# Four batches' inverse roots by Newton's steps on GpSimd, statistics tile by tile, and tokens normalized one tick earlier

## The chip, the cores and the metric

The kernel runs on one core of a Trainium2 chip. The metric is the device time of one execution in microseconds (us); the median of several runs counts. The engines are TensorE (PE; its weight loads are listed as PEld), VectorE (DVE), ScalarE (ACT), GpSimd (POOL) and SyncE (SP), which issues the DMAs. Each works through its own instruction queue in order; they wait for one another by semaphores.

## What is computed

Two layers on x of 8 batches x 256 tokens x 256 channels, all in float32: cross-attention with 16 heads of 16, a soft mixture of experts, a second cross-attention with 16 heads of 64, and a channel mix. Each takes a layer norm of x and adds its result to x:

```python
def _layernorm(x, axis=-1, eps=1e-05):
    m = jnp.mean(x, axis=axis, keepdims=True)
    v = jnp.var(x, axis=axis, keepdims=True)
    return (x - m) / jnp.sqrt(v + eps)

x = x + _L0_xattn_ref(_layernorm(x), ctx_768, mask_BxS2_bf1, ...)
x = x + _L0_ffn_ref(_layernorm(x), ...)
x = x + _L1_xattn_ref(_layernorm(x), ctx_768, ...)   # the second attention
x = x + _L1_ffn_ref(_layernorm(x), ...)              # the channel mix

# the channel mix, on xn = _layernorm(x)
x_prev = xn shifted by one token
xr = mu_r * xn + (1 - mu_r) * x_prev;  xk = mu_k * xn + (1 - mu_k) * x_prev
out = sigmoid(xr @ W_r.T) * (square(relu(xk @ W_k.T)) @ W_v.T)
```

The change touches the layer norms of the last two lines only: the normalized tokens that the second attention projects to queries, and the statistics (mean, variance, inverse root) of the channel mix.

## The kernel before

x stays on the chip as 16 tiles of 128 tokens (`x_sb`); batch b has tiles 2b and 2b+1. The four stages follow one another; in the profile the experts end at about 900 us, the second attention runs from about 930 to 1300, and the channel mix follows.

**The second attention** works through 64 steps, one for each batch and pair of heads (`steps1`, L1195). Two steps make a group, so a batch has four groups. The loop over ticks n (L1426) runs a software pipeline: in tick n it emits the scores of group n, the scaling of group n-1, the transposes of group n-2, the values of group n-3, and, after a batch's last group, its output projection (`project`). A batch's 4 ticks are called a block here.

- `scores` (L1217, L1222): PE writes scores to PSUM, VectorE takes their negated maxima `nm`, ScalarE the exponentials `ex`, four of 128x256 for each step, with their sums `z`.
- `norm` (L1233, L1235): VectorE takes the reciprocals `rz`, GpSimd multiplies `ex` by them, 128x1024 at a time.
- `transposes` (L1251): PE transposes `ex`; VectorE copies one half of each step to `et`, ScalarE the other.
- `values` (L1270): PE multiplies by the values, ScalarE copies the result to `ot`.
- `project` (L1283): PE multiplies by the output weights, VectorE adds the result to `x_sb`. With that a batch's rows are final; the projection of batch b is emitted in tick 4b+7.

Between these, each tick emits pieces for the next batch: keys (L1122, L1123: one half copied by ScalarE, the other by VectorE), values (L1187, L1188) and, in the first tick of a block, `xt_piece`: the two tiles of the next batch are normalized on VectorE (`normed`, L177, tile `xh_l1`), transposed on PE (`pt_x`) and copied to `xT` (L1137); four query pieces (L1157) follow over the block.

Three PSUM tiles of 128x512 (tag "mm") go round among transposes, keys, values, queries and projections, so a PE instruction that starts a new one waits until the copy that read the tile three turns earlier is done.

**Statistics of the channel mix.** `bn_stats` and `bn_aggr` on VectorE give a tile's mean and variance. For the first four batches `ln_half(0, ...)` is emitted at tick 20: eight pairs (L117, L118), one square root with epsilon as bias on ScalarE (L120), one reciprocal on VectorE (L121). The exponentials and the square root need different tables on ScalarE, so a table load stands ahead of the root and another ahead of the next exponential. For batches 4 to 6 `rest_of_stats(4, 3)` does the same at tick 33 (L1415 to L1421), and `rest_of_stats(7, 1)` after the loop. The mix itself (`channel_mix`) begins with `normed` (tile `xh_ffn`) and transposes.

**What sets the order.** The framework does not keep the order of emission: its scheduler orders each engine's queue by its own estimate of when operands are ready. Only what stands in `tc.keep_in_program_order` (PE's matmuls and transposes through `matmul` and `transpose`, `rz`, the roots at L1419) keeps its place. In the built program of before, the pairs of `bn_stats` and `bn_aggr` of batches 0 to 3 stand apart in VectorE's queue, each batch's after its projection's add, and the `xh_ffn` tiles of batches 0 and 1 follow soon after the reciprocal.

Of the kernel before, what the change touches and what calls it, by code (L numbers as in the profile page):

```python
# [7 lines left out]

F32 = mybir.dt.float32
U8 = mybir.dt.uint8  # L10
AF = mybir.ActivationFunctionType
ALU = mybir.AluOpType
AX = mybir.AxisListType

P = 128
B, S, D, C = 8, 256, 256, 192
# [6 lines left out]
EPS = 1e-5  # L23
# [39 lines left out]
def kernel(ctx: ExitStack, tc: tile.TileContext, a: dict, out: bass.AP):  # L63
    nc = tc.nc

    const = ctx.enter_context(tc.tile_pool(name="const", bufs=1))
    stat = ctx.enter_context(tc.tile_pool(name="stat", bufs=2))
# [25 lines left out]
    x_sb = const.tile([P, NT, D], F32, name="x_sb")  # L93
# [7 lines left out]
    epsb = const.tile([P, 1], F32, name="epsb")  # L101
# [7 lines left out]
            a["x"][P * n : P * (n + of), :].rearrange("(t p) d -> p t d", p=P),  # L109
        )  # L110

    def ln_half(half, name):

        mv = stat.tile([P, 8, 2], F32, tag="mv", name=f"mv_{name}")
        for i in range(8):
            st = stat.tile([P, 6], F32, tag="bst", bufs=4, name=f"bst_{name}_{i}")
            nc.vector.bn_stats(st, x_sb[:, half * 8 + i, :])  # L117
            nc.vector.bn_aggr(mv[:, i, :], st)  # L118
        rstd = stat.tile([P, 8], F32, tag="rstd", name=f"rstd_{name}")
        nc.scalar.activation(rstd, mv[:, :, 1], AF.Sqrt, bias=epsb)  # L120
        nc.vector.reciprocal(rstd, rstd)  # L121
        return mv, rstd

    def ln_tiles(n, of, name):

        mv = stat.tile([P, 4, 2], F32, tag="mvp", bufs=4, name=f"mvp_{name}")
        for i in range(of):
            st = stat.tile([P, 6], F32, tag="bst", bufs=4, name=f"bst_{name}_{i}")
            tc.keep_in_program_order(nc.vector.bn_stats(st, x_sb[:, n + i, :]))
            nc.vector.bn_aggr(mv[:, i, :], st)  # L130
        rstd = stat.tile([P, 4], F32, tag="rstdp", bufs=4, name=f"rstdp_{name}")
        nc.scalar.activation(rstd[:, :of], mv[:, :of, 1], AF.Sqrt, bias=epsb)
        nc.vector.reciprocal(rstd[:, :of], rstd[:, :of])
        return mv, rstd

    def ln_pair(p, name):
        return ln_tiles(4 * p, 4, name)
# [34 lines left out]
    def normed(b, mv, scl, name, of=8):  # L172

        xh = work.tile([P, 2, D], F32, tag="xh", bufs=3, name=f"xh_{name}_{b}")
        for t in range(2):
            i = (2 * b + t) % of
            nc.vector.tensor_scalar(  # L177
                xh[:, t, :],
                x_sb[:, 2 * b + t, :],
                mv[:, i, 0:1],  # L180
                scl[:, i : i + 1],
                ALU.subtract,
                ALU.mult,
            )
        return xh

    def transposed(xh, name, turn=None):

        pt = ps_mm(f"pt_{name}")
        for c in range(2):  # L190
            for t in range(2):
                (turn or free_transpose)(
                    pt[:, c * 256 + t * P : c * 256 + (t + 1) * P],
                    xh[:, t, c * P : (c + 1) * P])
        return pt.rearrange("p (c n) -> p c n", c=2)
# [27 lines left out]
    with ExitStack() as l0:  # L223
# [376 lines left out]
        for p in range(1, 4):  # L600
            h, b = 16 * (p - 1), 2 * p
# [160 lines left out]
        for b, plan in enumerate(  # L762
# [8 lines left out]
            for step in plan.split():  # L771
                when, _, args = step[1:].partition(".")
# [3 lines left out]
        turn_back, halves = None, []  # L776
        for h in range(8 * B + 12):
            q, k = [
                (i // 8, i % 8 // 2, i % 2) if 0 <= i < 8 * B else None for i in (h, h - 6)
            ]  # L780
# [284 lines left out]
    with ExitStack() as l1:  # L1065
# [61 lines left out]
        def proj1(b):  # L1127

            to = {}

            def xt_piece():
                mv, rstd = xat_stats[b // 2]
                pt = transposed(normed(b, mv, rstd, "l1", of=4), f"x1_{b}", transpose)
                to["xT"] = p1.tile([P, 2, S], F32, tag="xT", bufs=1, name=f"xT1_{b}")
                nc.vector.tensor_copy(to["xT"], pt)  # L1137
                for t in range(2):
                    nc.gpsimd.tensor_tensor(
                        x_sb[:, 2 * b + t, :], x_sb[:, 2 * b + t, :], bo, ALU.add  # L1140
                    )

            def q_piece(t2):
                if t2 == 0:
                    to["QT"] = p1.tile([P, 8, S], F32, tag="QT", bufs=2, name=f"QT1_{b}")
                pq = ps_mm(f"q1_{b}_{t2}").rearrange("p (t n) -> p t n", t=2)
                for i in range(2):
                    t = 2 * t2 + i
                    for c in range(2):
                        matmul(  # L1150
                            pq[:, i, :],
                            lhsT=wq[:, c, t * P : (t + 1) * P],
                            rhs=to["xT"][:, c, :],
                            start=(c == 0),
                            stop=(c == 1),
                        )
                nc.vector.tensor_scalar(  # L1157
                    to["QT"][:, 2 * t2 : 2 * t2 + 2, :], pq, HD1**-0.5, None, ALU.mult
                )

            def values_of(u):

                if u == 0:
                    to["V"] = p1.tile([P, 2, DA], F32, tag="V", bufs=2, name=f"V1_{b}")
                pv = [ps_mm(f"v1_{b}_{u}_{h}") for h in range(2)]
                t0 = S * b + u * P
                cols = [slice(h * 512, (h + 1) * 512) for h in range(2)]
                for h in range(2):
                    matmul(
                        pv[h],  # L1170
                        lhsT=ctx0T[:, t0 : t0 + P],
                        rhs=wv[:, 0, cols[h]],
                        start=True,
                        stop=False,
                    )

                def halves():
                    for h in range(2):
                        r = slice(64 * h, 64 * h + 64)
                        matmul(  # L1180
                            pv[h],
                            lhsT=ctx1T[r, t0 : t0 + P],
                            rhs=wv[r, 1, cols[h]],
                            start=False,
                            stop=True,
                        )
                    nc.scalar.copy(to["V"][:, u, cols[0]], pv[0])  # L1187
                    nc.vector.tensor_copy(to["V"][:, u, cols[1]], pv[1])  # L1188

                return halves  # L1190

            qs = [[xt_piece]] + [[lambda t=t: q_piece(t) for t in ts] for ts in ((0,), (1,), (2, 3))]
            return to, qs, [lambda u=u: values_of(u) for u in range(2)]

        def steps1(b, to):  # L1195

# [101 lines left out]
                if k < len(step):  # L1298
                    step[k]()

        to, qs, vs = projs[0]
        for t2 in range(4):
            keys(0, t2)()
        for v in vs:
# [4 lines left out]

        ffn_stats = {}
        homes = []

        def homes_of_mix():
# [8 lines left out]
        def channel_mix(b):  # L1324
# [81 lines left out]

            return mix, mixed_keys, mixed_values


        def rest_of_stats(b, of):  # L1410
            mv = stat.tile([P, 8, 2], F32, tag="mv", name=f"mv_ffn_{b}")
            rstd = stat.tile([P, 8], F32, tag="rstd", name=f"rstd_ffn_{b}")
            for i in range(2 * of):
                st = stat.tile([P, 6], F32, tag="bst", bufs=4, name=f"bst_ffn_{b}_{i}")
                nc.vector.bn_stats(st, x_sb[:, 2 * b + i, :])  # L1415
                nc.vector.bn_aggr(mv[:, (2 * b + i) % 8, :], st)
            part = slice(2 * b % 8, 2 * b % 8 + 2 * of)
            tc.keep_in_program_order(
                nc.scalar.activation(rstd[:, part], mv[:, part, 1], AF.Sqrt, bias=epsb)  # L1419
            )  # L1420
            nc.vector.reciprocal(rstd[:, part], rstd[:, part])  # L1421
            for k in range(b, b + of):
                ffn_stats[k] = mv, rstd, 8

        mixes = [channel_mix(b) for b in range(B)]
        for n in range(len(groups) + 4):  # L1426
            b, i = n // 4 + 1, n % 4
            stage(3, n - 3)
            if b < B:
                for piece in projs[b][1][i]:  # L1430
                    piece()
            stage(4, n - 4)
            stage(2, n - 2)
            stage(1, n - 1)


            if i < 2 and n // 8 < B // 2 - 1:
                keys(n // 8 + 1, n % 8 // 4 * 2 + i)()
            elif i >= 2 and b < B:
                projs[b][2][i - 2]()()  # L1440
            stage(0, n)
            if n == 20:
                mv, rstd = ln_half(0, "ffn_0")
                for k in range(4):
                    ffn_stats[k] = mv, rstd, 8
            if n == 33:
                homes_of_mix()
                mixes[0][0]()
                rest_of_stats(4, 3)
            if n == 34:  # L1450
                mixes[1][0]()
        rest_of_stats(7, 1)
        for k in range(1, B + 2):
            for i in range(3):
# [64 lines left out]
```

## Time and profile before

| | us |
|---|---|
| three runs without profiler | 1360.43, 1361.24, 1363.24 |
| their median | 1361.24 |
| the profiled execution | 1366.39 |
| its span, first to last instruction | 1364.6 |
| busy in it: TensorE | 1324.8 |
| VectorE | 571.0 |
| ScalarE | 582.0 |
| GpSimd | 192.8 |
| 69 table loads on ScalarE, each | 1.283 |

The mean granted clock of TensorE in the profiled execution was 0.989 of full speed. Times of single instructions below are those of the profiled execution, counted from the start of its span. A line of a timeline gives start, duration, engine, source line, operation, output<-inputs, shapes, how many instructions are merged in it, and in brackets how long the engine stood idle before it and for whom.

### The profile page before, as it was taken

How to read it: one execution, taken by the hardware profiler on the slowest of the kernel's cores; microseconds unless marked ns; L12 is line 12 of the kernel's file. 1: busy time of each engine (PE TensorE's matmuls, PEld its weight loads, DVE VectorE, ACT ScalarE, POOL GpSimd, SP SyncE). 2: the span in 40 equal slices, each digit the busy share in tenths (PEclk: the TensorE clock that was granted, in tenths of full speed). 3: DMA queues.
4: the chain of work that ended last, by engine and by line, in shares of the span. 5: the costliest groups of instructions: out<-in, count | busy, mean ns of one | idle time of the engine just before them, and what ended most of it. 6: DMA issues, size and time to landing. Idle time of an engine off the chain costs nothing.

```text
span 1364.6 us, 18968 instructions
## 1 busy us (share of the span) xinstructions
PE 1324.8 (97%) x7504; PEld 958.8 (70%) x7504; DVE 571.0 (42%) x1160; ACT 582.0 (43%) x1403; POOL 192.8 (14%) x142
## 2 busy tenths in 40 slices
PE   7998999899999999999999999999999999999998
PEld 3565565467678877778777788875666676677777
DVE  6577776523331133321333110015445444544565
ACT  2455444626342164522545222213536445444663
POOL 1000001101010000100001000002333323323433
PEclk8999998999999999999999999999999999999999
DMA  7100000023243324233233324450000000000001
GB/s 219 57 1 2 1 1 1 1 97 132 66 132 131 127 71 131 93 106 130 80 117 131 111 87 153 144 150 1 1 1 1 1 1 1 1 1 1 2 8 54
DMA packets 59128, 86.84 MB, mean 64 GB/s; under 512 B 3360, under 2 KB 49056, under 8 KB 59040
## 3 DMA queue, kind: packets, MB, share of 16 engines
q1 hardware_dynamic: 58464, 85.11, 19.2%
q8 instruction: 59, 0.97, 0.3%
q10 hardware_dynamic: 576, 0.52, 0.1%
q14 instruction: 29, 0.24, 0.1%
HBM read 83.53 MB, written 2.10 MB: 63 GB/s over the span
## 4 chain that ended last, share of the span: by engine, by line
PE 87%; ACT 6%; DVE 5%; issue 1%; DMA 0%; POOL 0%; ACTq 0%; SPq 0%; DVEq 0%; POOLq 0%
PE ph L968 16%; PE pe L984 16%; PE sc L73 8%; PE q L73 6%; PE o L73 5%; PE k L73 5%; PE po L73 5%; PE pc L1010 4%; PE pe L76 4%; PE v L73 4%; PE pf L914 3%; PE ln L832 3%; ACT ex L1222 2%; PE pf L73 1%; ACT ex L501 1%; DVE NM L490 1%
## 5 line engine op out<-in xcount | busy, mean ns | idle before, releaser
L976 ACT ACTIVATE ht<-ph,b 128x256 f32<-128x256 f32 x256 | 119.1, 473 | 372.1 <-PE ph L968 371.7
L968 PE MATMUL ph<-slots,w 128*128 128x256 f32 x1024 | 266.9, 384 | 0.9 <-ACT ht L976 0.2
L984 PE MATMUL pe<-w,ht 128*128 128x256 f32 x1024 | 263.3, 381 | 0.0
L968 PEld LDWEIGHTS ph<-slots,w 128*128 128x128 f32 x1024 | 182.3, 189 | 54.5 <-ACT ht L976 21.8
L984 PEld LDWEIGHTS pe<-w,ht 128*128 128x128 f32 x1024 | 192.0, 190 | 29.9 <-DVE slots L993 4.3
L1235 POOL TENSOR_TENSOR ex<-ex,rz 128x1024 f32<-128x1024 f32 x64 | 120.1, 1897 | 224.2 <-DVE rz L1233 214.0
L1222 ACT ACTIVATE ex<-sc,nm 128x256 f32<-128x256 f32 x256 | 117.2, 483 | 45.5 <-DVE nm L1217 45.5
L501 ACT ACTIVATE ex<-sc 128x512 f32<-128x512 f32 x128 | 74.7, 596 | 86.6 <-PE sc L73 76.1
L73 PE MATMUL sc<-KT,QT 17*128 17x256 f32 (+1 forms) x1024 | 105.3, 385 | 2.1 <-ACT QT L445 1.5
L490 DVE TENSOR_REDUCE NM<-sc 128x2 f32<-128x512 f32 x128 | 86.6, 687 | 41.4 <-PE sc L73 36.9
L993 DVE TENSOR_TENSOR slots<-pe,b 128x512 f32<-128x512 f32 x32 | 22.1, 691 | 185.4 <-PE pe L984 185.4
L73 PE MATMUL q<-xT,wq 128*128 128x256 f32 x384 | 94.8, 395 | 0.9 <-ACT V L1187 0.9
L73 PEld LDWEIGHTS sc<-KT,QT 17*128 17x128 f32 (+1 forms) x1024 | 77.4, 189 | 25.4 <-issue 15.9
L73 PEld LDWEIGHTS q<-xT,wq 128*128 128x128 f32 x384 | 70.9, 192 | 26.4 <-issue 12.9
L892 POOL TENSOR_TENSOR es<-es,zs 128x1024 f32<-128x1024 f32 x12 | 22.7, 1892 | 445.6 <-DVE zs L891 445.6
L1217 DVE TENSOR_REDUCE nm<-sc 128x4 f32<-128x1024 f32 x64 | 75.3, 1218 | 6.5 <-PE sc L73 2.8
L73 PE MATMUL po<-wo,ot 128*128 128x256 f32 x320 | 72.5, 382 | 0.0
L76 PE MATMUL pe<-ident,ex 128*128 128x128 f32 x512 | 69.9, 278 | 0.5 <-DVE xT L1137 0.4
L73 PEld LDWEIGHTS po<-wo,ot 128*128 128x128 f32 x320 | 60.1, 190 | 10.9 <-issue 3.2
L1251 ACT COPY et<-pe 128x512 f32<-128x512 f32 x64 | 37.0, 607 | 71.9 <-PE pe L76 71.5
L76 PEld LDWEIGHTS pe<-ident,ex 128*128 128x128 f32 x512 | 56.2, 140 | 14.0 <-issue 8.0
L73 PE MATMUL o<-et,V 128*64 128x256 f32 x512 | 62.8, 386 | 0.9 <-ACT ot L1270 0.9
(194 smaller groups left out, 1636.8 us busy)
## 6 DMA issues: line engine op xcount, KB each, us to landing
w<-in_w_dram SPq DMA_DIRECT2D x64, 1024.0 KB, 7.0
b<-in_b_dram SPq DMA_DIRECT2D x32, 128.0 KB, 6.8
x_sb<-in_x_dram SPq DMA_DIRECT2D x3, 512.0 KB, 7.3
ctx0T<-in_ctxT_dram SPq DMA_DIRECT2D x4, 256.0 KB, 8.4
ctx1T<-in_ctxT_dram SPq DMA_DIRECT2D x8, 128.0 KB, 6.9
se<-in_slots_dram SPq DMA_DIRECT2D x1, 1024.0 KB, 5.7
wq<-in_wq_dram SPq DMA_DIRECT2D x1, 1024.0 KB, 4.9
wo<-in_wo_dram SPq DMA_DIRECT2D x1, 1024.0 KB, 14.9
```

The source lines that it names most:

```text
L73: tc.keep_in_program_order(nc.tensor.matmul(out, lhsT=lhsT, rhs=rhs, start=start, stop=stop))
L76: tc.keep_in_program_order(nc.tensor.transpose(out, in_, ident))
L490: nc.vector.tensor_reduce(NMs[(2 * b + t // 2) % 2][:, qb, t, HD0 + 1 + 64 * i : 64 * i + 64 : 32], sc[i][:, :, 0, :], AX.X, ALU.max, nega ...
L501: nc.scalar.activation(ex[:, 2 - 2 * i : 4 - 2 * i, :], sc[1 - i][:, :, 1, :], AF.Exp)
L832: nc.tensor.matmul(pl[:, m * 512 : (m + 1) * 512], lhsT=st["xnT"][:, c, t * P : (t + 1) * P], rhs=snT[:, c, m * 512 : (m + 1) * 512], star ...
L968: nc.tensor.matmul(ph, lhsT=c_["w1"][:, c, hc * P : (hc + 1) * P], rhs=slots[e][:, c * 256 : (c + 1) * 256], start=(c == 0), stop=(c == 1),)
L976: nc.scalar.activation(ht, ph, AF.Gelu, bias=b1[:, e, hc : hc + 1])
L984: nc.tensor.matmul(c_["pe"][:, b, :], lhsT=c_["ht"][hc][:, b * SL : (b + 1) * SL], rhs=c_["w2"][:, hc, :], start=(hc == 0), stop=(hc == HI ...
L1010: nc.tensor.matmul(pc[:, :D], lhsT=CT[:, bl, e, t * P : (t + 1) * P], rhs=eos[e][:, bl, :], start=(e == 0), stop=(e == E - 1),)
L1217: nc.vector.tensor_reduce(nm, sc, AX.X, ALU.max, negate=True)
L1222: nc.scalar.activation(ex[:, i, qb, :], sc[:, i, qb, :], AF.Exp, bias=nm[:, i, qb : qb + 1], accum_out=z[:, i, qb : qb + 1],)
L1235: nc.gpsimd.tensor_tensor(ex, ex, rz.rearrange("p h q -> p (h q)").unsqueeze(2).to_broadcast([P, 4, S]), ALU.mult,)
```

## The change

- The eight pairs of statistics of batches 0 to 3, and the pairs of batches 4 to 7, are emitted one tile at a time: tile t of batch b at tick 4b+8+t, except those of batch 7, which come after the loop. All batches of a half share one tile of means and variances and one of inverse roots.
- The inverse roots of batches 0 to 3 are taken in tick 22 by `mix_roots`: GpSimd adds epsilon; VectorE makes a first guess from the bits (shift right by one, subtract from a constant, on the int32 view); GpSimd refines it by three Newton steps of four operations on 128x8. ScalarE's square root and VectorE's reciprocal for these batches are gone. Those of batches 4 to 7 are taken as before.
- The tokens of a batch are normalized for the second attention at the end of the last tick of the preceding block, instead of just ahead of their transposes.

```diff
-    def ln_half(half, name):
-        mv = stat.tile([P, 8, 2], F32, tag="mv", name=f"mv_{name}")
-        for i in range(8):
-            st = stat.tile([P, 6], F32, tag="bst", bufs=4, name=f"bst_{name}_{i}")
-            nc.vector.bn_stats(st, x_sb[:, half * 8 + i, :])
-            nc.vector.bn_aggr(mv[:, i, :], st)
-        rstd = stat.tile([P, 8], F32, tag="rstd", name=f"rstd_{name}")
-        nc.scalar.activation(rstd, mv[:, :, 1], AF.Sqrt, bias=epsb)
-        nc.vector.reciprocal(rstd, rstd)
-        return mv, rstd
+    def inverse_root(y, v, name):
+        n = v.shape[1]
+        t = stat.tile([P, 8], F32, tag="nt", bufs=1, name=f"nt_{name}")[:, :n]
+        nc.vector.tensor_scalar(
+            t.bitcast(I32), v.bitcast(I32), 1, None, ALU.logical_shift_right
+        )
+        nc.vector.tensor_scalar(
+            y.bitcast(I32), t.bitcast(I32), -1.0, float(0x5F3759DF), ALU.mult, ALU.add
+        )
+        for _ in range(3):
+            nc.gpsimd.tensor_tensor(t, y, y, ALU.mult)
+            nc.gpsimd.tensor_tensor(t, t, v, ALU.mult)
+            nc.gpsimd.tensor_scalar(t, t, -0.5, 1.5, ALU.mult, ALU.add)
+            nc.gpsimd.tensor_tensor(y, y, t, ALU.mult)
...
+            def normed_piece():
+                mv, rstd = xat_stats[b // 2]
+                to["xh"] = normed(b, mv, rstd, "l1", of=4)
+
             def xt_piece():
-                mv, rstd = xat_stats[b // 2]
-                pt = transposed(normed(b, mv, rstd, "l1", of=4), f"x1_{b}", transpose)
+                pt = transposed(to["xh"], f"x1_{b}", transpose)
...
-        to, qs, vs = projs[0]
+        to, qs, vs, of_batch = projs[0]
+        of_batch()
+        projs[1][3]()
...
+        halves = [
+            (
+                stat.tile([P, 8, 2], F32, tag="mv", name=f"mv_ffn_{k}"),
+                stat.tile([P, 8], F32, tag="rstd", name=f"rstd_ffn_{k}"),
+            )
+            for k in range(2)
+        ]
+        ffn_stats = [(*halves[b // 4], 8) for b in range(B)]
+
+        def mix_stats(b, t):
+            st = stat.tile([P, 6], F32, tag="bst", bufs=4, name=f"bst_ffn_{b}_{t}")
+            nc.vector.bn_stats(st, x_sb[:, 2 * b + t, :])
+            nc.vector.bn_aggr(halves[b // 4][0][:, (2 * b + t) % 8, :], st)
+
+        def mix_roots():
+            mv, rstd = halves[0]
+            v = stat.tile([P, 8], F32, tag="nv", bufs=1, name="nv_ffn")
+            nc.gpsimd.tensor_scalar(v, mv[:, :, 1], EPS, None, ALU.add)
+            inverse_root(rstd, v, "ffn")
 
         def rest_of_stats(b, of):
-            mv = stat.tile([P, 8, 2], F32, tag="mv", name=f"mv_ffn_{b}")
-            rstd = stat.tile([P, 8], F32, tag="rstd", name=f"rstd_ffn_{b}")
-            for i in range(2 * of):
-                st = stat.tile([P, 6], F32, tag="bst", bufs=4, name=f"bst_ffn_{b}_{i}")
-                nc.vector.bn_stats(st, x_sb[:, 2 * b + i, :])
-                nc.vector.bn_aggr(mv[:, (2 * b + i) % 8, :], st)
+            mv, rstd = halves[1]
             part = slice(2 * b % 8, 2 * b % 8 + 2 * of)
...
             stage(0, n)
-            if n == 20:
-                mv, rstd = ln_half(0, "ffn_0")
-                for k in range(4):
-                    ffn_stats[k] = mv, rstd, 8
+            if i == 3 and b + 1 < B:
+                projs[b + 1][3]()
+            if n >= 8 and i < 2 and n < 34:
+                mix_stats(n // 4 - 2, i)
+            if n == 22:
+                mix_roots()
             if n == 33:
                 homes_of_mix()
                 mixes[0][0]()
                 rest_of_stats(4, 3)
             if n == 34:
                 mixes[1][0]()
+        for t in range(2):
+            mix_stats(7, t)
         rest_of_stats(7, 1)
```

In the built program after the change, the queues of TensorE and SyncE hold the same instructions in the same order as before. VectorE's queue around the roots reads, in order: the last two pairs of statistics (batch 3), the two integer operations, the copy of V (L1188), two `xh_ffn` tiles, two maxima `nm`, the copies `xT` and `et`. GpSimd's thirteen operations stand after the products `ex` of batch 4's steps 4 and 5 and ahead of those of steps 6 and 7. The two key tiles of the tick (`k1_3_2_0` and `k1_3_2_1`) have changed what they wait for: before, the first waited for VectorE and the second for ScalarE; now it is the other way round.

More of the change, by code (lines that the diff above doesn't have):

```diff
@@ L9 @@
 F32 = mybir.dt.float32
+I32 = mybir.dt.int32
 U8 = mybir.dt.uint8
@@ L1192, in proj1 @@
             qs = [[xt_piece]] + [[lambda t=t: q_piece(t) for t in ts] for ts in ((0,), (1,), (2, 3))]
-            return to, qs, [lambda u=u: values_of(u) for u in range(2)]
+            return to, qs, [lambda u=u: values_of(u) for u in range(2)], normed_piece
         def steps1(b, to):
@@ L1308 @@
                 piece()
-        ffn_stats = {}
         homes = []
@@ L1421, in rest_of_stats @@
             nc.vector.reciprocal(rstd[:, part], rstd[:, part])
-            for k in range(b, b + of):
-                ffn_stats[k] = mv, rstd, 8
         mixes = [channel_mix(b) for b in range(B)]
@@ L1441 @@
             stage(0, n)
-            if n == 20:
-                mv, rstd = ln_half(0, "ffn_0")
-                for k in range(4):
-                    ffn_stats[k] = mv, rstd, 8
+            if i == 3 and b + 1 < B:
[4 more added lines that the diff above has]
+                mix_roots()
             if n == 33:
```

## The prediction

> **What bounds the kernel now.** I read the page first, then the timeline of the matrix engine (PE) over the second attention, then the timelines of the other engines at the one place where PE loses time there, last the order of instructions of the two built programs.
>
> ```profile
> PE 1324.8 (97%) x7504; PEld 958.8 (70%) x7504; DVE 571.0 (42%) x1160; ACT 582.0 (43%) x1403; POOL 192.8 (14%) x142
> PEclk8999998999999999999999999999999999999999
> PE 87%; ACT 6%; DVE 5%; issue 1%; DMA 0%; POOL 0%; ACTq 0%; SPq 0%; DVEq 0%; POOLq 0%
> ```
>
> PE sets the end: 97% busy, 87% of the chain. What happens elsewhere counts only where PE stands still for it. In the second attention (about 930 to 1300 us) PE stands still for some 0.8 us once a block, in the tick in which a batch's tokens are transposed, and once for more, at 1175 to 1179.5:
>
> ```profile
> 1127.04 1.98 PE L73 MATMUL k<-ctx0T,wk 128*128 128x512 f32 x4 [0.77 <-ACT et L1251]
> 1128.96 1.13 PE L73 MATMUL k<-ctx1T,wk 64*128 64x512 f32 x4
> ...
> 1175.23 1.16 PE L76 MATMUL pe<-ident,ex 128*128 128x128 f32 x8 [0.42 <-DVE xT L1137]
> 1176.66 1.13 PE L73 MATMUL k<-ctx0T,wk 128*128 128x512 f32 x2 [0.26 <-DVE et L1251]
> 1179.50 1.13 PE L73 MATMUL k<-ctx0T,wk 128*128 128x512 f32 x2 [1.71 <-ACT et L1251]
> 1180.56 1.13 PE L73 MATMUL k<-ctx1T,wk 64*128 64x512 f32 x4
> ```
>
> The second place is where the four batches' roots are taken. The other engines there (timelines of VectorE, ScalarE and GpSimd):
>
> ```profile
> 1167.75 0.18 DVE L118 BATCH_NORM_AGGREGATE mv_ffn<-bst_ffn 128x2 f32<-128x6 f32 x1
> 1169.30 0.20 DVE L121 RECIPROCAL rstd_ffn<-rstd_ffn 128x8 f32<-128x8 f32 x1 [1.37 <-ACT rstd_ffn L120]
> 1169.54 2.09 DVE L177 TENSOR_SCALAR xh_ffn<-x_sb,mv_ffn,rstd_ffn 128x256 f32<-128x256 f32 x2
> 1171.55 0.68 DVE L1188 COPY V<-v 128x512 f32<-128x512 f32 x1
> 1172.15 2.34 DVE L1217 TENSOR_REDUCE nm<-sc 128x4 f32<-128x1024 f32 x2
> ...
> 1167.67 1.28 ACT L120 ACT_TABLE_LOAD   x1
> 1173.44 1.28 ACT L1222 ACT_TABLE_LOAD   x1 [3.07 <-DVE nm L1217]
> 1174.73 0.47 ACT L1222 ACTIVATE ex<-sc,nm 128x256 f32<-128x256 f32 x1
> ...
> 1167.41 3.74 POOL L1235 TENSOR_TENSOR ex<-ex,rz 128x1024 f32<-128x1024 f32 x2 [15.25 <-DVE rz L1233]
> ```
>
> To see: the maxima `nm` of the scores start at 1172.15, behind the normalization `xh_ffn` in VectorE's queue; the exponentials then wait for a table load of 1.28; ScalarE's copy `et` comes after eight of them; PE waits for that copy. One block earlier the same tick has neither roots nor loads:
>
> ```profile
> 1120.95 2.35 DVE L1217 TENSOR_REDUCE nm<-sc 128x4 f32<-128x1024 f32 x2
> ...
> 1122.28 0.47 ACT L1222 ACTIVATE ex<-sc,nm 128x256 f32<-128x256 f32 x1 [1.61 <-DVE nm L1217]
> ```
>
> From the start of its scores to the second half of the keys it takes 1128.96 - 1119.88 = 9.08 us; the tick with the roots 1180.56 - 1169.59 = 10.97. So all that this place can give is 1.89 us.
>
> **The change, part by part.** The order of the two built programs tells most. PE's and SP's orders are unchanged. VectorE's statistics stand in the same places: before, the scheduler had already moved each tile's pair up to the moment its rows were ready.
>
> ```profile
> L118 DVE BATCH_NORM_AGGREGATE mv_ffn<-bst_ffn x8: 150/167/182, 1018.1 to 1167.7; 128x2 f32<-128x6 f32 x8
> ```
>
> Tile-by-tile statistics: 16 pairs before, 16 after, 0 us; were their cover gone, 8 x (0.41 + 0.17) = 4.6 us on VectorE. The tokens `xh_l1`: same places too, and no PE row waits for them, 0 us; uncovered, 0.73 for two tiles by 8 batches, 5.8 us. No DMA moves. The second half's roots stay on ScalarE, 0 us.
>
> What differs is the first half's roots. Gone: two table loads (2 x 1.28), a square root (0.30, L120) on ScalarE, a reciprocal (0.20) on VectorE. New: two 128x8 operations on VectorE and thirteen on GpSimd: one that adds epsilon (`nv`), and three rounds of three products and one tensor-scalar, each waiting for the one before. VectorE's queue now reads: last aggregate, the two integer operations (waiting for `nv`), copy of V, `xh_ffn` (waiting for the last of the thirteen), `nm`, `nm`, `xT`, `et`. Behind `xh_ffn` stand the maxima that the exponentials need, and the copies that free PE's banks.
>
> Step by step. GpSimd reaches `nv` when its two `ex` products are done, 1167.41 + 3.74 = 1171.15. `nv` takes about 0.15 (between the memset of 128x2, 0.10, and the product below); a handover between engines takes 0.08 (ScalarE's relu ends 1318.64, GpSimd's square starts 1318.72). The two integer operations: 0.17 each (128x8 tensor-scalar, L333) and 0.04 between (1169.50 to 1169.54). So V's copy starts at 1171.76, against 1171.55, and GpSimd's twelve at 1171.84.
>
> One small GpSimd product is in no row. From below: a memset of 128x2 takes 0.10, with 0.03 between (VectorE's gap to itself), 0.13. From above: L1139's 128x256 takes 0.74, less 248 elements at 1.64 ns (128x256 at 641 to 128x1024 at 1897), 0.33, and 0.08, 0.41. I take the line through those two rows at 8 elements, 0.23 (through 128x512 at 1039 it is 0.19), so 0.20, and 0.08 for the wait; the tensor-scalar 0.15 and 0.08: 9 x 0.28 + 3 x 0.23 = 3.2 us. Bounds: 12 x 0.13 = 1.6 and 12 x 0.41 = 4.9.
>
> Then: chain done 1175.04, handover, two `xh_ffn` in 0.73 (GpSimd now idle; in the trace the first of the two took 1.77 beside `ex`), so `nm` starts at 1175.85, 3.70 later than now. Exponentials 1.33 after it, as one block earlier: 1177.18, 2.45 later than now, since the load is gone. From them to PE's keys 4.76 (1122.28 to 1127.04): 1181.94; to the keys' second half 1.92: 1183.86 against 1180.56. The last step costs 0.86 more than now, because the order of banks turns: the first key tile now waits for ScalarE's copy and the second for VectorE's; before it was the reverse, and one tile ran inside the stall. Sum: +3.3 us; with the bounds, +1.7 to +5.0. PE has no later stall until 1297 that could absorb it.
>
> The Trainium skill ("ScalarE: Activation LUTs", What ACT_TABLE_LOAD costs) adds a drain of 1.38 us to each load. Here the square root starts 0.02 after its load ends, so the rows do not show it. As an estimate from the page, the reload removed would be worth 1.4 more and the sum +1.9.
>
> PE would have no full matmul from 1173.3 to 1181.9: transposes for some 2.7 us, else idle. The clock in the trace shows what such stretches do:
>
> ```profile
> 212.00:217.00 5.00, 2.80 (x30) 1.70 (x24) 3.65 (x8) 3.11 (x11) 1.03 (x2) 1.00 0.00 0
> 217.00:225.00 8.00, 8.00 (x40) 4.35 (x40) 2.86 (x8) 1.84 (x4) 1.07 (x1) 0.57 0.00 0
> ```
>
> (Columns: stretch, length, PE, PE's loads, VectorE, ScalarE, GpSimd busy, clock, DMA.) After a stretch of transposes and gaps the clock was 0.57 for 8 us, at 269 to 276 it was 0.53 for 7: 3.4 us of full-speed work lost. From below 0: in the present stall (2.4 us idle) the clock held at 1.00. Here part of the slow time falls into the stall itself; I take 1.3, bounds 0 and 3.4.
>
> The skill's rule ("TensorE: Matmul & The Clock Gate", Part 1) is that an idle window of about 3.4 us halves the clock until a busy one has passed. It speaks against this change: as an estimate from the page, 8.6 us hold at least one whole window, and each slow window of full work costs 1.7 us.
>
> Total +4.6 us. The profiled execution took 1366.39 (span 1364.6 and 1.8 around it), 0.4% above the median of 1361.24; a local sum carries over unscaled: 1365.8.
>
> **The rivals.**
> 1. Short chain, clock held: each step 0.13 to 0.2 and no drop. +1.6 to +2.4, taken as 1363.2. For it: the memset's 0.10, and no drop since 276. Against: three of four steps are products with two inputs.
> 2. Long chain: steps of 0.41 and a clock drop, +5.0 + 3.4 at most, taken as 1368.5. For it: GpSimd's waits for itself in the trace (start-up memsets) lie behind other work, so its turnaround is unseen.
> 3. Not slower: the chain costs nothing because `nm` does not really stand behind it. PE then repeats the tick of one block earlier, -1.9: 1359.3. It decides if the twelve end by 1172.0, under 0.02 us each; for it speaks that memsets start 0.03 apart, against it that each product waits for the last.
> 4. The scheduler leaves this place as it was: excluded by the order of the programs.
>
> **How the numbers follow.** The forecast 0.64, short chain 0.15, long chain 0.13, not slower 0.08. A measurement here tells about 0.2% from no change, 2.7 us. The forecast lies above that but for 0.03 of its share; the long chain adds its 0.13: slower 0.74. Short chain, that 0.03 and half of "not slower", 0.22: same. Faster 0.04, since a gain over 2.7 is more than the place holds. The range goes from the chain's lower bound with no drop, +1.7, less the 0.8 by which the lowest run lies under the median, 1362.0, to 1369.0, +7.8 of the +8.4 that both upper bounds make; it leaves out the end of the long chain and most of "not slower". The forecast's own range is 1363.9 (steps of 0.22, no drop) to 1367.9 (+3.3 and +3.4).
>
> **What will show it.** Right: thirteen small rows on GpSimd around 1171 to 1175 (by before's times), 0.2 to 0.3 us apart; `xh_ffn` waiting for them; one PE stall of some 3 to 4 us before `xT`'s bank and one of 2 before `et`'s; PE's clock under 1 in the 7 us after. Wrong: `nm` starting before 1173; a new stall in another tick; PE idle less than 2.4 us there. Falsified as a whole if the time is below 1361.

## The result, and the profile after

| | before | after |
|---|---|---|
| median, us | 1360.93 (11 runs, 1359.26 to 1366.02) | 1367.15 (11 runs, 1365.01 to 1371.31) |
| ratio of the times | | 1.0037, 95% interval 1.0023 to 1.0052 |
| span of the profiled execution | 1364.6 | 1365.6 |
| scores of the tick with the roots, to the next values | 13.75 | 19.61 |
| those scores to the end of the span | 195.0 | 201.0 |

The change costs 5 to 6 us: 1.0037 of 1361 is 5.0, the medians differ by 6.2. The two spans differ by 1.0 only, because TensorE's clock dropped differently in their first 300 us (read in 1-us windows, some 31 us at half speed before, some 17 after), and the scores of this tick start 5.0 us earlier after the change (1164.61 against 1169.59). So from here on a tick is measured from the start of its own scores, the row `sc` in which batch 4's steps meet the roots. From there to the end the changed kernel takes 201.0 - 195.0 = 6.0 us more, and 19.61 - 13.75 = 5.86 of it lie in the one tick.

The engines' sums of the page show nothing of it (first lines of section 1, 2 and 4 after the change):

```profile
PE 1323.1 (97%) x7504; PEld 959.7 (70%) x7504; DVE 571.2 (42%) x1161; ACT 579.0 (42%) x1400; POOL 195.6 (14%) x155
PEclk9999999999999999999999999999999999899999
PE 87%; ACT 6%; DVE 5%; issue 1%; POOL 1%; DMA 0%; SPq 0%; ACTq 0%; DVEq 0%; POOLq 0%
```

ScalarE is 3.0 us less busy, GpSimd 2.8 more with 13 instructions more; the only trace of the loss is the digit 8 in the clock's row. The timeline of PE after the change:

```profile
1164.61 1.89 PE L74 MATMUL sc<-KT,QT 64*128 64x256 f32 x16
...
1168.80 1.04 PE L77 MATMUL pe<-ident,ex 128*128 128x128 f32 x8
1174.08 1.94 PE L77 MATMUL pe<-ident,ex 128*128 128x128 f32 x8 [4.24 <-DVE xT L1146]
1177.06 3.78 PE L74 MATMUL k<-ctx0T,wk 128*128 128x512 f32 x4 [1.05 <-ACT et L1260]
1180.77 1.80 PE L74 MATMUL k<-ctx1T,wk 64*128 64x512 f32 x4
1182.40 1.89 PE L74 MATMUL sc<-KT,QT 64*128 64x256 f32 x16
1184.22 1.95 PE L74 MATMUL o<-et,V 128*64 128x256 f32 x16
```

PE waits 4.24 us for VectorE's copy `xT` (0.42 before), then 1.05 for ScalarE's `et`. The keys start 12.45 us after the scores, and then need 3.78 for what took 1.98 elsewhere. GpSimd's, VectorE's and ScalarE's timelines after the change say why:

```profile
1162.44 3.74 POOL L1244 TENSOR_TENSOR ex<-ex,rz 128x1024 f32<-128x1024 f32 x2 [15.25 <-DVE rz L1242]
1166.26 0.24 POOL L1438 TENSOR_SCALAR nv_ffn<-mv_ffn 128x8 f32<-128x8 f32 x1
1166.99 0.20 POOL L137 TENSOR_TENSOR nt_ffn<-rstd_ffn 128x8 f32<-128x8 f32 x1 [0.49 <-DVE rstd_ffn L133]
1167.28 0.20 POOL L138 TENSOR_TENSOR nt_ffn<-nt_ffn,nv_ffn 128x8 f32<-128x8 f32 x1
1167.57 0.20 POOL L139 TENSOR_SCALAR nt_ffn<-nt_ffn 128x8 f32<-128x8 f32 x1
...
1170.10 0.20 POOL L140 TENSOR_TENSOR rstd_ffn<-rstd_ffn,nt_ffn 128x8 f32<-128x8 f32 x1
```

```profile
1166.53 0.17 DVE L130 TENSOR_SCALAR nt_ffn<-nv_ffn 128x8 int32<-128x8 int32 x1 [3.58 <-POOL nv_ffn L1438]
...
1170.33 0.73 DVE L183 TENSOR_SCALAR xh_ffn<-x_sb,mv_ffn,rstd_ffn 128x256 f32<-128x256 f32 x2 [2.83 <-POOL rstd_ffn L140]
1170.99 2.34 DVE L1226 TENSOR_REDUCE nm<-sc 128x4 f32<-128x1024 f32 x2
1173.25 0.68 DVE L1146 COPY xT<-pt_x 128x512 f32<-128x512 f32 x1
```

```profile
1172.30 0.47 ACT L1231 ACTIVATE ex<-sc,nm 128x256 f32<-128x256 f32 x1 [6.91 <-DVE nm L1226]
```

Twelve dependent operations of 0.20, started 0.28 apart; `xh_ffn` waits 2.83 for the last of them, and behind it stand `nm`, `xT` and the exponentials. The windows of the tick (columns: stretch, length, busy time of PE, its loads, VectorE, ScalarE, GpSimd, then the granted clock) show the rest:

```profile
1164.60:1169.80 5.20, 5.20 (x46) 3.71 (x42) 0.94 (x3) 0.58 (x1) 3.82 (x12) 1.00 0.00 0
1169.80:1171.90 2.10, 0.04 (x1) 0.00 (x0) 1.57 (x3) 0.00 (x0) 0.40 (x2) 1.00 0.00 0
1171.90:1182.15 10.25, 7.03 (x16) 3.59 (x18) 5.80 (x9) 5.20 (x19) 3.79 (x2) 0.50 0.01 3
1182.15:1186.00 3.85, 3.85 (x34) 2.40 (x30) 3.05 (x3) 1.78 (x6) 0.00 (x0) 1.00 0.00 0
```

PE's clock is halved for 10.2 us, and 5.1 of these come after the keys have started. At full clock it takes 4.70 us from a block's keys to its next values; here it took 1184.22 - 1177.06 = 7.16. So the tick's 5.86 are 3.40 for the later start of the keys (12.45 + 4.70 - 13.75) and 2.46 for the clock.

### The profile page after: what moved, and what is told of

Read it like the earlier page. It is cut to its first block, busy times and chain, and to the rows that moved or that the text cites. A ratio compares the mean times of both kernels' runs of the same rounds, so it can differ in the third digit from the quotient of the medians.

```text
span 1365.6 us, 18975 instructions
## 1 busy us (share of the span) xinstructions
PE 1323.1 (97%) x7504; PEld 959.7 (70%) x7504; DVE 571.2 (42%) x1161; ACT 579.0 (42%) x1400; POOL 195.6 (14%) x155
## 4 chain that ended last, share of the span: by engine, by line
PE 87%; ACT 6%; DVE 5%; issue 1%; POOL 1%; DMA 0%; SPq 0%; ACTq 0%; DVEq 0%; POOLq 0%
PE ph L974 16%; PE pe L990 16%; PE sc L74 8%; PE q L74 6%; PE o L74 5%; PE po L74 5%; PE k L74 5%; PE pc L1016 4%; PE v L74 4%; PE pe L77 4%; PE pf L920 3%; PE ln L838 3%; ACT ex L1231 2%; DVE NM L496 1%; PE pf L74 1%; ACT ex L507 1%
```

## The experiments

My theory: only the wait of `nm` behind the chain costs, and the clock it brings down; statistics tile by tile and earlier tokens cost nothing. Rivals: one of the other edits costs; the chain's length doesn't matter; the clock doesn't. The table has what each kernel's profiled execution showed: keys' start after the scores (K), keys to next values (V), scores to next values (S), scores to the end of the span (E), in us, and the ratio to the kernel before with its interval.

| | K | V | S | E | ratio |
|---|---|---|---|---|---|
| before | | | 13.75 | 195.0 | 1 |
| the change | 12.45 | 7.16 | 19.61 | 201.0 | 1.0037 (1.0023 to 1.0052) |
| roots on ScalarE | | | 13.75 | 195.0 | 0.9996 (0.9978 to 1.0013) |
| two steps | 11.33 | 7.72 | 19.05 | 200.4 | 1.0023 (1.0008 to 1.0038) |
| five steps | 14.71 | 6.09 | 20.80 | 202.2 | 1.0045 (1.0029 to 1.0061) |
| filled | 12.49 | 4.70 | 17.19 | 198.6 | 1.0017 (1.0003 to 1.0031) |
| five steps, filled | 14.71 | 6.11 | 20.82 | 202.1 | 1.0049 (1.0035 to 1.0063) |
| `xh_ffn` later | 8.90 | 4.70 | 13.60 | 195.7 | 0.9997 (0.9982 to 1.0012) |
| and epsilon on VectorE | 8.39 | 4.70 | 13.09 | 195.1 | 1.0001 (0.9987 to 1.0016) |
| root in tick 31 | 7.16 | 4.70 | 11.86 | 195.0 | 1.0010 (0.9995 to 1.0026) |
| root in tick 32 | 7.17 | 4.70 | 11.87 | 194.0 | 0.9998 (0.9984 to 1.0012) |
| the change, again | 12.46 | 7.13 | 19.59 | 201.0 | 1.0050 (1.0034 to 1.0067) |
| the change, a third time | 12.49 | 7.02 | 19.51 | 200.9 | one execution |

(Before and with the roots on ScalarE, the two key tiles start apart, so they have no one K.)

**One part alone: the roots back on ScalarE.** The rest of the change stays.

```diff
 def mix_roots():
-    v = stat.tile([P, 8], F32, tag="nv", bufs=1, name="nv_ffn")
-    nc.gpsimd.tensor_scalar(v, mv[:, :, 1], EPS, None, ALU.add)
-    inverse_root(rstd, v, "ffn")
+    nc.scalar.activation(rstd, mv[:, :, 1], AF.Sqrt, bias=epsb)
+    nc.vector.reciprocal(rstd, rstd)
```

> The change without its roots: statistics tile by tile and tokens normalized early stay, the four batches' roots go back to ScalarE's square root and VectorE's reciprocal. The built queues are then those of the kernel before. My theory (only the roots cost): ratio to before 1.000; from the start of the tick's scores to the start of the next tick's scores 11.9 us, as in before. Rival (the statistics or the tokens, in their new form, carry part of the loss): ratio 1.001 to 1.004.

The tick is that of the kernel before, row by row on PE, its stalls of 0.42, 0.26 and 1.71 included. PE's timeline in this run:

```profile
1169.66 1.16 PE L77 MATMUL pe<-ident,ex 128*128 128x128 f32 x8 [0.42 <-DVE xT L1146]
1171.09 1.12 PE L74 MATMUL k<-ctx0T,wk 128*128 128x512 f32 x2 [0.26 <-DVE et L1260]
1173.92 1.12 PE L74 MATMUL k<-ctx0T,wk 128*128 128x512 f32 x2 [1.71 <-ACT et L1260]
```

So statistics tile by tile and earlier tokens cost nothing that can be measured, and the Newton roots make the whole loss.

**The chain's length: two steps and five.** Eight and twenty chained operations in place of twelve (with two, the roots are less exact); the second kernel has `range(5)`.

```diff
-        for _ in range(3):
+        for _ in range(2):
```

> The changed kernel with two Newton steps instead of three (the roots are less exact), all other instructions in the same order. My theory (VectorE's queue waits for the whole chain, 0.28 us an operation): maxima nm 1.12 us earlier against the scores, the tick 16.7 us if the clock still falls to half (ratio 1.0037), 14.2 if it holds (1.0018); after has 17.8. Rival (the chain's length does not matter, only that VectorE waits for GpSimd at all, or the order of banks): 17.8, ratio 1.0045.

> The changed kernel with five Newton steps and nothing filled in. My theory: the same wait as with the filled stall, and the clock falls to half in it; scores to next values 19.4 plus 1.2 to 3.5 for the clock, 20.6 to 22.9 (after: 19.6). Two steps gave 19.05, only 0.56 less than three, since the clock was low for about 10 us there and not 10.2 minus the shorter wait; so single executions can differ by a window of the clock. Rival (the clock's price grows with the wait): above 22.9.

The keys start at 11.33, 12.45 and 14.71 with 8, 12 and 20 operations: 1.12 / 4 = 0.28 and 2.26 / 8 = 0.28 us for each. The chain is on the path with its full length. The time from scores to values does not follow: one step less saves 0.56 instead of 1.12, two more cost 1.19 instead of 2.26, since the clock takes back part of it (V is 7.72, 7.16, 6.09).

**The clock alone: matmuls that fill the wait.** Four matmuls of 128x512 are written into a tile ahead of its transposes, which overwrite them; a second kernel has five steps and seven such matmuls.

```diff
+                        if tag == "1_4_4" and i == 1:
+                            for _ in range(4):
+                                matmul(
+                                    pt.rearrange("p c q -> p (c q)"),
+                                    lhsT=ident,
+                                    rhs=wq[:, 0, 0:512],
+                                    start=True,
+                                    stop=True,
+                                )
```

> The changed kernel with four more matmuls of 128x512 (3.8 us of PE work whose result is overwritten) in the stall, ahead of the transposes of batch 4's step 4. My theory (the clock falls because PE has no full matmul for two windows, and that costs 2.4 us beyond the wait): clock 1.00 throughout, keys at full speed, the tick 15.3 us, ratio 1.002, so the kernel gets faster by added work. Rival (the loss is the wait alone, the clock's fall is hidden in it): tick 17.8 or more, ratio 1.0045 or more.

> The kernel with the filled stall, but five Newton steps (eight more GpSimd operations) and seven extra matmuls instead of four, so that the clock has no reason to fall. My theory (with the clock held, each GpSimd operation in the chain costs its 0.28 us on PE): from the start of the tick's scores to the start of the next tick's values 17.2 + 8 x 0.28 = 19.4 us, the clock at 1.00, ratio about 1.004. Rival (operations of the chain are worth less than their own time, because something else ends last): 17.2 to 18.5.

With three steps PE has 3.6 us more to do, and E is shorter than the change's by 201.0 - 198.6 = 2.4 us. The ratios, 1.0017 against 1.0037 and 1.0050, lie the same way (the interval overlaps the first one's and not the second's). PE's timeline in that run (the trace has two entries for each of these matmuls):

```profile
1171.48 3.60 PE L74 MATMUL pe<-wq,ident 128*128 128x512 f32 x8
...
1176.34 1.16 PE L77 MATMUL pe<-ident,ex 128*128 128x128 f32 x8 [0.82 <-DVE xT L1146]
1179.34 1.98 PE L74 MATMUL k<-ctx0T,wk 128*128 128x512 f32 x4 [1.83 <-ACT et L1269]
1181.25 1.13 PE L74 MATMUL k<-ctx1T,wk 64*128 64x512 f32 x4
```

The keys start where they did (12.49), but take 1.98 and V is 4.70: the clock held. That is the price of the clock alone, 2.4 us. With five steps the fill missed: the clock fell after it, the run gained nothing on five steps without a fill, and its S of 20.82 lies above both what I expected (19.4) and the rival (17.2 to 18.5). The windows of that run:

```profile
1168.00:1174.00 6.00, 6.00 (x20) 2.97 (x18) 2.15 (x4) 0.19 (x1) 2.75 (x14) 1.00 0.00 0
1174.00:1178.00 4.00, 2.27 (x14) 1.34 (x12) 3.55 (x8) 4.00 (x18) 0.49 (x1) 1.00 0.02 6
1178.00:1181.45 3.45, 2.87 (x4) 1.17 (x4) 0.00 (x0) 1.01 (x3) 3.26 (x2) 0.51 0.00 0
```

The fill ended at 1174.5; in the 4 us after it PE had transposes and stalls, and the half-speed stretch of 3.4 us lay over the keys, which cost as much as the long stretch had (V 6.11 against 6.09).

**The place in the queue: `xh_ffn` taken out of the way.** The normalized tiles of batches 0 to 2 are emitted in ticks 24 to 26 and kept in that order; the chain stays as it is.

```diff
-    def normed(b, mv, scl, name, of=8):
+    def normed(b, mv, scl, name, of=8, kept=False):
...
+            if kept:
+                tc.keep_in_program_order(done)
...
+                xh = early.get(b) or normed(b, mv, rstd, "ffn", of=of)
...
+            if n in (24, 25, 26):
+                mv, rstd, of = ffn_stats[n - 24]
+                early[n - 24] = normed(n - 24, mv, rstd, "ffn", of=of, kept=True)
```

> The changed kernel, with xh_ffn of the first three batches emitted at ticks 24, 25 and 26 and kept there, so that no maxima stand behind it; the thirteen GpSimd operations and VectorE's two stay where they are. My theory: VectorE still waits for the epsilon operation behind GpSimd's two products, nm starts 2.8 us after the scores' start (2.6 before, 6.4 after), the tick 11.8 us with the clock at 1.00, ratio 1.000. Rival (the thirteen operations themselves, or contention for SBUF by them, cost): most of the 6 us stays, ratio over 1.003.

The twelve operations run as before, and the loss is gone from the tick: S 13.60, ratio 0.9997. (E stays 0.7 above before: one block later PE now waits 0.61 for `xT`, which stands behind two pairs of `xh_ffn` tiles at their new place.) VectorE's timeline in that run:

```profile
1168.89 0.17 DVE L130 TENSOR_SCALAR nt_ffn<-nv_ffn 128x8 int32<-128x8 int32 x1 [3.59 <-POOL nv_ffn L1443]
...
1169.77 2.34 DVE L1228 TENSOR_REDUCE nm<-sc 128x4 f32<-128x1024 f32 x2
```

`nm` no longer waits for the chain, only for its start: the two integer operations stand ahead of it and wait for `nv`, which on GpSimd stands behind 3.74 us of `ex` products. With the `ex` row above this splits the wait in two: `nm` started 6.38 after the scores with both, 2.82 without the chain. The run also tells that these roots can be used two to four ticks later at little cost.

**A better version, first try: epsilon on VectorE too.** On top of the moved `xh_ffn`, so that nothing before `nm` waits for GpSimd's queue.

```diff
-            nc.gpsimd.tensor_scalar(v, mv[:, :, 1], EPS, None, ALU.add)
+            nc.vector.tensor_scalar(v, mv[:, :, 1], EPS, None, ALU.add)
```

> Newton's roots with neither wait: xh_ffn of three batches kept at ticks 24 to 26, and epsilon added on VectorE instead of GpSimd, so that VectorE waits for nothing there. My theory: nm starts 1.1 us after the scores' start as in the block before, scores to next values 11.9 us (before 13.75), the clock at 1.00, the tiles xh_ffn cost nothing at their new places: ratio 0.9987. Rival (Newton on GpSimd costs something wherever it is): ratio 1.000 or above.

It missed: `nm` started at 2.31 and not at 1.1. VectorE's timeline in that run, beside GpSimd's `ex` products of 1161.70 to 1165.44:

```profile
1162.25 1.37 DVE L1443 TENSOR_SCALAR nv_ffn<-mv_ffn 128x8 f32<-128x8 f32 x1
1163.65 1.82 DVE L130 TENSOR_SCALAR nt_ffn<-nv_ffn 128x8 int32<-128x8 int32 x1
1165.50 0.17 DVE L133 TENSOR_SCALAR rstd_ffn<-nt_ffn 128x8 int32<-128x8 int32 x1
```

Two operations on eight elements last until 1163.62 and 1165.47, near the middle and the end of GpSimd's two products; the third, after them, takes 0.17. The wait for GpSimd had only changed its form. One block later the `xh_ffn` tiles at their new place last as long beside GpSimd's products (2.28 and 1.75 for two, against 0.73), and the copy `xT` behind them is late for PE, which waits 0.61 for it at 1220.65. S is 0.66 less than before, 0.61 goes again there, and E is no better than before.

**A better version, second try: no Newton, the square root late.** ScalarE's root for the four batches, kept in order in tick 31 (a second kernel: 32) in place of 22, where the other batches' root needs the same table anyway.

```diff
-            v = stat.tile([P, 8], F32, tag="nv", bufs=1, name="nv_ffn")
-            nc.gpsimd.tensor_scalar(v, mv[:, :, 1], EPS, None, ALU.add)
-            inverse_root(rstd, v, "ffn")
+            tc.keep_in_program_order(nc.scalar.activation(rstd, mv[:, :, 1], AF.Sqrt, bias=epsb))
+            nc.vector.reciprocal(rstd, rstd)
...
-            if n == 22:
+            if n == 31:
                 mix_roots()
```

> No Newton: the four batches' square root stays on ScalarE but is emitted at tick 31, after the last exponentials, next to the later batches' roots, so that two table loads go (one load of the root's table, one reload of the exponentials'). My theory: scores to next values 11.9 us as in the block before, clock 1.00; at the end of the attention the load, the root and five or six xh_ffn tiles stand in slack or cost up to 1 us: ratio 0.9986 to 0.9994. Rival (the tail is as tight as the tick was): 1.000 or above.

> As the run with the square root at tick 31, but emitted one tick later, so that in ScalarE's queue it stands behind the copies ot and et of the last exponentials, where ScalarE stood idle for 1.5 us. There the earlier run won its 1.89 us at the roots' old place (11.86 from scores to next values) and lost 1.6 of it again, since the table load stood ahead of a copy ot that PE waited for (2.49 us idle instead of 0.88). My theory: the 11.86 stays, PE waits 0.9 for that copy, and up to 0.5 is lost where PE waits for the first xh_ffn: ratio 0.9986 to 0.9992. Rival (no place at the end is free): 0.9996 or above.

Both make the tick that of an undisturbed block, S 11.86 and 11.87: the 1.89 us are real. In tick 31 they are lost again at the end, as the rival had it (ratio 1.0010). ScalarE's and PE's timelines in that run:

```profile
1294.37 1.28 ACT L1437 ACT_TABLE_LOAD   x1
1295.66 0.30 ACT L1437 ACTIVATE rstd_ffn<-mv_ffn,epsb 128x8 f32<-128x8 f32 x1
1295.87 0.57 ACT L1279 COPY ot<-o 128x512 f32<-128x512 f32 x1
```

```profile
1296.49 2.43 PE L74 MATMUL o<-et,V 128*64 128x256 f32 x16 [2.49 <-ACT ot L1279]
```

The load stands ahead of a copy that PE waits for, 2.49 us instead of 0.88. One tick later it stands behind it, and PE waits 0.89. Instead it loses 0.9 around the first `xh_ffn` (from these products to the next, 5.76 against 4.82 before; 0.53 of it shows as a wait), and E is 194.0, 1.0 less than before. By the times that is undecided: 0.9998 with an interval of 0.9984 to 1.0012 holds my 0.9986 to 0.9992 and the rival's 0.9996. No kernel here is shown to beat the one before.

**The clock again.** The changed kernel, executed twice more with a profile.

> The changed kernel once more, for the clock: the windows in which the clock is judged lie differently in each execution, so by my theory the keys start 12.45 us after the scores again, and from the keys to the next values it takes between 4.7 (clock held) and 8.2 (a whole window lost); the first look had 7.16. Rival (the clock's loss is fixed by the kernel): 7.16 again. Ratio 1.003 to 1.005.

> A third execution of the changed kernel, for the clock alone. In the first two the half-speed stretch began 7.31 and 7.25 us after the scores' start and lasted 10.2 us in both, and from the keys to the next values it took 7.16 and 7.13 us. My theory (the judging windows' phase against the kernel is free): keys again at 12.45, but a beginning elsewhere, and keys to next values away from 7.1 by over 0.3. Rival (PE's idle time itself sets the beginning, some 2 us after PE falls idle): 7.25 +- 0.2 and 7.1 +- 0.1 a third time.

My theory, that at this place the windows lie differently in each execution, fell. V was 7.16, 7.13, 7.02. Windows of a quarter of a us place the half-speed stretch, counted from the scores' start:

| | begins | ends | length | V above 4.70 |
|---|---|---|---|---|
| the change | 7.31 | 17.55 | 10.24 | 2.46 |
| again | 7.24 | 17.48 | 10.24 | 2.43 |
| third time | 10.48 | 17.31 | 6.83 | 2.32 |
| two steps | 7.31 | 17.55 | 10.24 | 3.02 |
| five steps | 7.31 | 17.55 | 10.24 | 1.39 |
| five steps, filled | 14.17 | 17.58 | 3.41 | 1.41 |

The lengths are 3, 2 and 1 times 3.41. The third beginning is 3.2 us later than the first two, so the rival (PE's idle time sets the beginning) fell as well, though V hardly changed. For the end is nearly the same in all six, and what the stretch costs is half of what lies between the keys' start and its end: (17.55 - 12.45) / 2 = 2.55 against 2.46, with two steps 3.11 against 3.02, with five 1.42 against 1.39.

All the same the windows are not tied to the kernel. In the first execution of the change its half-speed stretches, those of the first 300 us too, end at 59.17, 127.44, 161.57, 219.60 and 1182.16 us from the span's start: 20, 10, 17 and 282 steps of 3.413 us apart, so on one grid. The other two executions have such a grid as well, but it lies elsewhere against the span's start: divided by 3.413, the ends leave 1.15, 0.08 and 0.88 us in the three. Yet the kernel arrives at this place at nearly the same point of the grid each time, within 0.3 us in the six. Why was not tried.

## Why the prediction was right

The direction, the place and the mechanism held; the forecast of 1365.8 lies 1.35 us under the median (as a ratio 1.0034 against 1.0037, within the interval), and the missing part is nearly all one term, the clock. By its steps, counted from the scores' start:

| step | forecast | measured |
|---|---|---|
| tile-by-tile statistics, earlier tokens | 0 | ratio 0.9996 (0.9978 to 1.0013) |
| GpSimd reaches `nv` | 1.56 | 1.65 |
| `nv` takes | 0.15 | 0.24 |
| the chain of twelve | 3.2 | 3.31 |
| `nm` starts | 6.26 | 6.38 |
| exponentials start | 7.59 | 7.69 |
| keys start | 12.35 | 12.45 |
| later keys, in the tick | 3.3 | 3.40 |
| the clock | 1.3 | 2.46 |
| all | 4.6 | 5.86 in the tick, 6.0 to the end |

- **The chain.** No row of before had a small GpSimd product; the forecast took 0.28 for a product, from the line through two larger ones, and 0.23 for the tensor-scalar, from a value between a memset and the product; all are 0.28. The lower bound (0.13) and the upper (0.41) are both refuted by the slope of three kernels.
- **What stands behind it.** The queue order of the built program was the step that mattered: it put `xh_ffn`, and so the chain, ahead of `nm`. With `xh_ffn` moved and the chain kept, the loss is gone.
- **The clock, the term that was mis-sized.** "Here part of the slow time falls into the stall itself; I take 1.3, bounds 0 and 3.4." That it would fall, and that part would be hidden, was right. The value between the bounds had no working, so that the total came near is in this part chance. The hidden part ends with the keys' start, what costs is half the rest, and the rest was 5.1 us in these executions: 2.5. The filled run takes this term away, and 2.4 us go with it.
- **Signs named in advance.** Thirteen small rows, the twelve of the chain 0.28 apart, `xh_ffn` waiting for them, the clock under 1: all there. The first PE stall is 4.24, a little over the 3 to 4 named. The second PE stall is 1.05 and not 2, because the transposes ahead of it ran at half clock, 1.94 instead of 1.16, and took up the rest of the wait for `et`; in the third execution, where they ran nearly all at full speed (1.21), it is 1.78.
- **Rivals.** Short chain with the clock held (1363.2): the chain isn't short, the clock fell in all three executions. Long chain (1368.5): refuted for the chain, half right for the clock. Not slower (1359.3): it needed `nm` free of the chain; the run that frees it gives 0.9997, not a gain, since the wait for `nv` remains.
- **The table loads.** The prediction's other estimate, with 1.4 us more for the reload that goes (+1.9 in place of +3.3), does not fit: the wait's part is 3.40.

## What to carry to other kernels

A chain of tiny dependent operations costs its number times its start-to-start time, whatever their size, and it costs it where its consumer's queue has work behind the consumer: read that queue in the built program, not the order of emission. Where PE's wait grows to several us, ask until when the clock stays low and charge half of what then lies behind the restart; a longer wait can so cost less than its length, and idle PE time filled with useless matmuls can pay (2.4 us here with three steps, nothing with five). Taking an engine out of a wait (here ScalarE's table loads) gains only if what replaces it is not ordered ahead of the same work.

## What the runs showed of the hardware

- A GpSimd operation on 8 elements for each partition takes 0.20 us in the trace (0.24 for the one that reads `mv`), and a dependent one starts 0.28 after it, product or tensor-scalar alike.
- A VectorE tensor-scalar on 128x8 took 1.82 us beside GpSimd's products and ended with them, and took 0.17 after them. The Trainium skill ("SBUF — State Buffer", Who interferes with whom) says that VectorE and GpSimd share a pair of ports that is held for a whole instruction, and counts tensor-scalar among the operations that can want it. The rows agree, down to eight elements.
- The half-speed stretches are whole multiples of 3.41 us. The Trainium skill ("TensorE: Matmul & The Clock Gate", Part 1) speaks of a free-running window of about 3.4 us, whose phase differs from run to run. The lengths agree, and so does the phase against the span's start (remainders of 1.15, 0.08 and 0.88 us in three executions of one kernel). Against this place it hardly varied, with ends at 17.3 to 17.6 us after the scores in six executions of four kernels; so in this case the clock's price was nearly the same each time (2.46, 2.43, 2.32).
- The clock did not fall in stalls of up to 2.5 us (2.49 in tick 31, 1.83 behind `et`), and not in the 4.4 us between the end of the fill (the start of the next row) and the keys in the filled run, with stalls of 0.82 and 1.83 in them; with 4.1 us after the longer fill it fell. What differs is where this time lies on the grid. The step of the grid that ended as the clock fell, 1174.63 to 1178.04, had PE busy for 1.64 us, with transposes alone; in the other run the step from 1174.22 to 1177.64 had 2.46 us, the end of the fill among them. A threshold of busy time does not follow: in the third execution of the change a step with 1.58 us let the clock stand.
